# A third inner product of seven in the gated projection, with partial sums put back into PSUM by ScalarE

## The chip, the cores and the metric

One core of a Trainium2 chip. The metric is the device time of one launch in microseconds. Five engines work beside each other, each in its own order and joined by semaphores: TensorE (PE, with its weight loads as PEld), VectorE (DVE), ScalarE (ACT), GpSimd (POOL) and SyncE (SP, which here issues DMAs). Everything is float32. The times of the kernel before are from 3 runs; every other number is from one profiled execution.

## The reference

A graph network on 1024 nodes of 512 features: a normalisation, a graph convolution, four layers, a second graph convolution, and sums with the input. A layer is an attention over a condition and then this block, the part that the change touches:

```python
u = _ln(h, ln3_w[i], ln3_b[i]) @ geglu_w[i] + geglu_b[i]     # 1024x512 @ 512x4096
val, gate = jnp.split(u, 2, axis=-1)
f = val * jax.nn.gelu(gate, approximate=False)               # 1024x2048
h = h + f @ ffo_w[i] + ffo_b[i]                              # 1024x2048 @ 2048x512
```

At the end, `x + (... + relu(layernorm(x)))` is needed once more; the kernel prepares that sum ("base") in eight blocks of 128 rows during the layers and keeps it in DRAM.

## The kernel before

**Sevens.** Most large products are made by Winograd's form of Strassen's scheme: a product of 2x2 blocks takes 7 block products in place of 8, with sums of blocks ahead of them (of weights, mostly on POOL) and sums of results behind them (on VectorE). The block products are numbered 0 to 6 in the order of `order7`.

**Rounds and quads.** The gated projection of a layer `l` goes in `R` = 4 rounds `r`, each for 512 value and 512 gate columns. The outer seven of a round has the blocks val/gate halves by node halves; its left blocks (`left[0..6]`, weights and their sums `ges`) are made by `geglu_weights` on POOL as soon as the round before has made its last sum (`geglu.last`, tile `fs`), its right blocks are `ln3T` and `ln3S`. A `Quad` is 128 of the 512 columns, `c` = 0 to 3: each outer block product of a quad is two matmuls 128x512 into one PSUM bank. Round 0 takes the quads one after the other (`Quad.rest`). Behind each round `ffn_out` multiplies the result `fT` by 512 rows of the output weights (`fa` to `fd`).

**Pairs.** In rounds 1 to 3 quads go in pairs, `p` = 0 (quads 0 and 2) and `p` = 1 (quads 1 and 3). For two of the outer block products, numbers 5 and 6 (`INNER`), a pair makes its four matmuls 128x512 as a seven of its own: `Pair.seven(i)` issues seven matmuls 128x256 into two banks, `ge` (halves a and b) and `gf` (halves c and d). It has two parts, divided by a `yield`:

- products 0 into a, 5 into b, 6 into c, 4 into d; ScalarE copies a to SBUF (L1025), VectorE adds b (L1027), c (L1029) and d (L1031) to that,
- products 1 onto a, 3 onto c, 2 onto d; ScalarE copies a (L1034), VectorE adds c (L1036) and d (L1038).

The results are two SBUF tiles `gw`, one for each quad of the pair. The blocks of blocks that this needs are made on POOL: the left ones by `inner_lefts` right behind `geglu_weights` (tiles `gi`), the right ones once a layer by `inner_right_of` during round 0 (tile `wos`, free at that time).

`Pair.run` weaves the two sevens with the outer products 0 and 4 of both quads, which are ordinary wide matmuls into banks `ga` and `gd`. VectorE adds `ga` and the results of the sevens in SBUF (L1052, L1061). `Quad.end` then makes the products 3, 2 and 1 (banks `gc`, `gd`, `ga`) and the gates: g1 and g0 are sums of a bank and an SBUF tile (L964, L968), gelu on ScalarE (L933), then value times gate (L971 to L975).

**What sets the order.** The tile framework gives every engine its own queue, orders instructions ahead of time by its own estimates, so that matmuls of one step can stand among those of another, and puts in the semaphores. PSUM has eight banks of 128x512, given out from one pool (`bank`). Weights are in 36 buffers (`slot`), loaded by SP; 512-wide scratch tiles are in 10 buffers (`t512`).

**Base blocks.** In rounds 1 to 3 of layer 0 and round 1 of layer 1, two blocks of x each are loaded again (`fetch_x`), normalised by ScalarE, added to the bias and to x by POOL, and written to DRAM through SP's queue (`base_of`).

Of the kernel before, what the change touches and what calls it, by code (L numbers as in the profile page):

```python
# [8 lines left out]
F32 = mybir.dt.float32  # L9
# [5 lines left out]
OP = mybir.AluOpType  # L15
AX = mybir.AxisListType

P = 128
# [5 lines left out]
def gnn_kernel(  # L24
# [46 lines left out]
    slots = ctx.enter_context(tc.tile_pool(name="slots", bufs=36))  # L71
    work = ctx.enter_context(tc.tile_pool(name="work", bufs=10))
    hpool = ctx.enter_context(tc.tile_pool(name="hpool", bufs=1))
    rows = ctx.enter_context(tc.tile_pool(name="rows", bufs=2))
    small = ctx.enter_context(tc.tile_pool(name="small", bufs=4))
    dram = ctx.enter_context(tc.tile_pool(name="dram", bufs=1, space=bass.MemoryType.DRAM))
    psum = ctx.enter_context(tc.tile_pool(name="psum", bufs=8, space=bass.MemoryType.PSUM))
# [14 lines left out]
    def bank(name):  # L92
        return psum.tile([P, 512], F32, tag="bank", name=name)

    def t512(name, dtype=F32):
        return work.tile([P, 512], dtype, tag="t512", name=name)

    def slot(name):
        return slots.tile([P, 2, 512], F32, tag="slot", name=name)
# [10 lines left out]
            )  # L110
        return w

    def load_row(vec, offset, name):
        t = rows.tile([P, D], F32, tag="row", name=name)
        nc.sync.dma_start(
            t, bass.AP(tensor=vec.tensor, offset=vec.offset + offset, ap=[[0, P], [1, D]])
        )
        return t
# [790 lines left out]
    class Quad:  # L909
# [49 lines left out]
        def end(self):  # L959

            n, c, bias = self.n, self.c, gcols[:, self.cv:self.cv + 1]
            pc, pd = bank(f"gc_{n}"), self.d
            g1 = t512(f"g1_{n}")
            nc.vector.tensor_tensor(g1, pd, self.u3, OP.add)  # L964
            self.gate(g1, n)
            self.product(3, pc, True)
            g0 = t512(f"g0_{n}")
            nc.vector.tensor_tensor(g0, pc, self.u3, OP.add)  # L968
            self.gate(g0, n)
            self.product(2, pd, False)  # L970
            nc.vector.scalar_tensor_tensor(self.u2, pd, bias, self.u2, OP.add, OP.add)  # L971
            f0, f1 = (self.fT[i][c // 2][:, c % 2, :] for i in range(2))
            nc.vector.tensor_tensor(f1, self.u2, g1, OP.mult)
            self.product(1, self.a, False)
            nc.vector.scalar_tensor_tensor(f0, self.a, bias, g0, OP.add, OP.mult)  # L975

# [6 lines left out]
    def inner_right(t, y, t1, t2, t3, t4):  # L983

        b11, b12, b21, b22 = (y[:, k, n * M:(n + 1) * M] for k in range(2) for n in range(2))
        for to, of, less in ((t1, b12, b11), (t3, b22, b12), (t2, b22, t1), (t4, b21, t2)):
            t.tensor_tensor(to, of, less, OP.subtract)
        return [b11, b21, b22, t4, t1, t2, t3]

    INNER = (5, 6)  # L990

    def inner_lefts(l, r, left):
        rooms = [t512(f"gi_{l}_{r}_{i}") for i in range(3)]
        rooms = [x[:, i * M:(i + 1) * M] for x in rooms for i in range(2)]
        return {i: inner_left(nc.gpsimd, left[i], *rooms[3 * n:3 * n + 3])
                for n, i in enumerate(INNER)}

    def inner_right_of(n, right):
        rooms = [wos[:, 2 * n + k, i * M:(i + 1) * M] for k in range(2) for i in range(2)]
        return inner_right(nc.gpsimd, right[INNER[n]], *rooms)  # L1000

    class Pair:

# [4 lines left out]
        def seven(self, i):  # L1010

            n, p = f"{self.n}_{i}", self.p
            left, right = (x[i] for x in self.inner)
            e, f = bank(f"ge_{n}"), bank(f"gf_{n}")
            a, b, c, d = e[:, :M], e[:, M:], f[:, :M], f[:, M:]
            t = acc_tile(f"gt_{n}")
            to = self.w = [acc_tile(f"gw{q}_{n}") for q in range(2)]
            s1, u2 = t[:, :M], t[:, M:]

            def product(k, to, start):  # L1020
                nc.tensor.matmul(to, left[k][:, p * P:(p + 1) * P], right[k], start=start,
                                 stop=True, skip_group_check=True)

            product(0, a, True)
            nc.scalar.copy(s1, a)  # L1025
            product(5, b, False)
            nc.vector.tensor_tensor(u2, b, s1, OP.add)  # L1027
            product(6, c, True)
            nc.vector.tensor_tensor(s1, c, u2, OP.add)  # L1029
            product(4, d, False)  # L1030
            nc.vector.tensor_tensor(to[1][:, M:], d, s1, OP.add)  # L1031
            yield
            product(1, a, False)
            nc.scalar.copy(to[0][:, :M], a)  # L1034
            product(3, c, False)
            nc.vector.tensor_tensor(to[1][:, :M], c, u2, OP.add)  # L1036
            product(2, d, False)
            nc.vector.tensor_tensor(to[0][:, M:], d, u2, OP.add)  # L1038
            yield

        def run(self, sums, beside):
            q0, q1 = self.quads
            for q in self.quads:
                q.a = bank(f"ga_{q.n}")
            q0.product(0, q0.a, True)
            steps = self.seven(5)
            next(steps)
            q1.product(0, q1.a, True)
            next(steps)
            for q, w in zip(self.quads, self.w):  # L1050
                q.u2 = w
                nc.vector.tensor_tensor(w, q.a, w, OP.add)  # L1052
            steps = self.seven(6)
            next(steps)
            for q in self.quads:
                q.d = bank(f"gd_{q.n}")
            q0.product(4, q0.d, True)
            next(steps)
            for q, w in zip(self.quads, self.w):
                q.u3 = w  # L1060
                nc.vector.tensor_tensor(w, w, q.u2, OP.add)  # L1061
            q1.product(4, q1.d, True)
            for q in self.quads:
                q.end()
                sums(q.c)
            beside(self.p)
# [196 lines left out]
    for l in range(L):  # L1263
# [119 lines left out]

        last = l == L - 1
        lnT = None
        kept = slot(f"kept_{l}")
        fetched, rights = {}, {}

# [14 lines left out]
        for r in range(R):  # L1403
            if r:
                wff = out_weights(nc.gpsimd, l, r, raw_out)
            else:
                raw_out = load_out(l, 0)
            if r + 1 < R:
                raw = load_geglu(l, r + 1)
            beside = lambda c: None  # L1410
            if r:
                fT, fS, quads = pairs_of(l, r, left, right, (lefts, rights))
                nb = 2 * (l * (R - 1) + r - 1)
                if nb < NB:
                    if nb == 0:
                        bias_out = load_row(gcn_out_b, 0, "bias_out")
                        nc.gpsimd.tensor_tensor(x_shift, x_mean.rearrange(
                            "p a (b c) -> p (a b) c", c=2)[:, :, 0], x_root, OP.mult)
                        nc.gpsimd.tensor_scalar(x_shift, x_shift, -1.0, None, OP.mult)
                    fetch_x(nb)  # L1420
                    fetch_x(nb + 1)
                    beside = lambda p: base_of(nb + p)
            else:
                wff = []

                def beside(c):
                    if c == 2:
                        wff.extend(out_weights(nc.vector, l, 0, raw_out))
                    elif c < 2:
                        with waiting_for(quads[c].last, mybir.EngineType.Pool):  # L1430
                            rights[INNER[c]] = inner_right_of(c, right)

            fT = geglu(quads, fT, fS, not r, beside)
            if r + 1 < R:
                raw_out = load_out(l, r + 1)
                with waiting_for(geglu.last, mybir.EngineType.Pool):
                    left = geglu_weights(l, r + 1, *raw)
                    lefts = inner_lefts(l, r + 1, left)
                    if not r:
                        for nb in range(NB - 2, NB):  # L1440
                            add_bias(nb)
                for s in range(2):
                    ffn_out(l, r, s, fT, wff, kept)
            else:
                lnT = [slots_of(2, f"ln2T_{l + 1}_{i}") for i in range(2)]
                if last:
                    w_out, base = load_last()
                else:
                    projections = load_projections(l + 1)
                ffn_out(l, r, 0, fT, wff, kept)  # L1450
                ready_first(l + 1, [0, 1, 4, 5])
                ffn_out(l, r, 1, fT, wff, kept)
                turn_first(l + 1, [0, 1, 4, 5])
                left_to_turn = [2, 3, 6, 7]
                ready_first(l + 1, left_to_turn[:2])
# [58 lines left out]
```

## Time and profile before

| | us |
|---|---|
| median of 3 runs | 2515.99 (2515.88 to 2517.99) |
| the profiled execution | 2517.15 |
| its span in the profile | 2515.4 |
| PE busy | 2488.1 |
| DVE busy | 1487.5 |
| POOL busy | 619.7 |
| ACT busy | 534.0 |

A MATMUL row of the trace is half of a float32 matmul, with its end modelled; the distance from one start to the next is what PE spends on it. PEld is the load of the stationary operand ahead of each half. A bracket at a row's end gives the idle time of its engine just before, and what ended it. Lines (L1021 and so on) are those of the kernel before; all matmuls of quads and of the other large products have the line of the helper `multiply`, L302.

### The profile page before, as it was taken

To read this page: it belongs to the slowest core of one execution; us is meant where nothing else is said; L and a number is where in the kernel's file an instruction comes from. 1 tells how busy PE (TensorE), PEld (TensorE's weight loads), DVE (VectorE), ACT (ScalarE), POOL (GpSimd) and SP (SyncE) were. 2 spreads that over 40 slices of the span, in tenths; PEclk is the share of its full clock that TensorE was granted. 3 is DMA by queue.
4 is the path that set the end of the run, shared out by engine and by line. 5 is a ranking of instruction groups with operands and counts; after the bars stand their busy time and mean duration, and the time that the engine had idled before them with its cause. 6 is when DMAs were issued, how large, how long until landed. Compare 5 with 4: busy or idle time off the path is not lost. (4 is left out here: it accounts for less than half of the span.)

```text
span 2515.4 us, 33075 instructions
## 1 busy us (share of the span) xinstructions
PE 2488.1 (99%) x12752; PEld 1821.3 (72%) x12752; DVE 1487.5 (59%) x3298; ACT 534.0 (21%) x1318; POOL 619.7 (25%) x581
## 2 busy tenths in 40 slices
PE   8999999999999999999999999999999999999998
PEld 5778886666668887566677888566677888566665
DVE  9655565566764555666574555655574555665561
ACT  7322222111112222111112222211112222211111
POOL 1322233444220113432420113133401112233300
PEclk9999999999999999999999999999999999999999
DMA  6302231121211112020202211110121112111210
GB/s 180 131 30 93 93 120 58 47 67 34 105 59 61 58 64 68 28 81 17 96 30 76 72 64 56 46 42 26 51 76 59 60 59 68 43 42 51 84 34 34
DMA packets 69380, 161.06 MB, mean 64 GB/s; under 512 B 5768, under 2 KB 6096, under 8 KB 69216
## 3 DMA queue, kind: packets, MB, share of 16 engines
q1 hardware_dynamic: 67120, 153.44, 18.7%
q0 software_dynamic: 1376, 4.30, 0.5%
q8 instruction: 105, 1.72, 0.3%
q10 hardware_dynamic: 720, 1.11, 0.1%
q14 instruction: 59, 0.48, 0.1%
HBM read 135.76 MB, written 23.07 MB: 63 GB/s over the span
## 5 line engine op out<-in xcount | busy, mean ns | idle before, releaser
L302 PE MATMUL ga<-ln3T,wval 128*128 128x512 f32 x512 | 245.6, 593 | 0.0
L302 PEld LDWEIGHTS ga<-ln3T,wval 128*128 128x128 f32 x512 | 96.0, 190 | 89.5 <-issue 85.1
L933 ACT ACTIVATE g<-g,gcols 128x512 f32<-128x512 f32 x128 | 87.3, 716 | 329.6 <-DVE g L946 112.6
L777 ACT ACTIVATE pr<-sc,nmax 128x256 f32<-128x256 f32 x256 | 118.2, 474 | 176.7 <-DVE nmax L772 176.7
L302 PE MATMUL gd<-ln3S,ges 128*128 128x512 f32 x256 | 128.1, 592 | 0.0
L302 PE MATMUL pa_v<-wv,ct 128*128 128x256 f32 x512 | 123.1, 379 | 0.0
L220 POOL TENSOR_TENSOR ges<-wgate,wgate 128x1024 f32<-128x1024 f32 x16 | 37.7, 2354 | 342.6 <-DVE fs L1087 329.0
L302 PE MATMUL fa<-wff,fT 128*128 128x256 f32 x512 | 121.6, 379 | 0.0
L302 PE MATMUL gd<-ln3T,ges 128*128 128x512 f32 x256 | 120.7, 594 | 0.6 <-DVE g L964 0.6
L302 PE MATMUL pc_v<-wv,ct 128*128 128x256 f32 x512 | 121.0, 379 | 0.0
L302 PE MATMUL pd_v<-wvs,ct 128*128 128x256 f32 x512 | 121.0, 379 | 0.0
L302 PE MATMUL pc_k<-ct,wk 128*128 128x256 f32 x512 | 120.9, 379 | 0.0
L302 PE MATMUL pd_k<-ct,wks 128*128 128x256 f32 x512 | 120.9, 379 | 0.0
L302 PE MATMUL gc<-ln3S,wgate 128*128 128x512 f32 x256 | 120.3, 592 | 0.0
L302 PE MATMUL pa_k<-ct,wk 128*128 128x256 f32 x480 | 116.2, 385 | 0.0
L302 PEld LDWEIGHTS fa<-wff,fT 128*128 128x128 f32 x512 | 97.3, 190 | 21.8 <-issue 9.1
L302 PEld LDWEIGHTS pc_k<-ct,wk 128*128 128x128 f32 x512 | 97.3, 190 | 13.2
L302 PEld LDWEIGHTS pd_k<-ct,wks 128*128 128x128 f32 x512 | 97.3, 190 | 13.2
L302 PEld LDWEIGHTS pd_v<-wvs,ct 128*128 128x128 f32 x512 | 97.3, 190 | 13.2
L302 PEld LDWEIGHTS pa_v<-wv,ct 128*128 128x128 f32 x512 | 97.1, 190 | 13.5 <-issue 0.4
L302 PEld LDWEIGHTS pc_v<-wv,ct 128*128 128x128 f32 x512 | 95.7, 190 | 12.2
L302 PEld LDWEIGHTS pa_k<-ct,wk 128*128 128x128 f32 x480 | 88.7, 190 | 21.3 <-issue 10.4
(354 smaller groups left out, 4971.5 us busy)
## 6 DMA issues: line engine op xcount, KB each, us to landing
ct<-cond_dram SPq DMA_DIRECT2D x72, 512.0 KB, 4.4
wval<-in_L_gnn_geglu_w_dram SPq DMA_DIRECT2D x32, 512.0 KB, 4.3
wgate<-in_L_gnn_geglu_w_dram SPq DMA_DIRECT2D x32, 512.0 KB, 4.8
wff<-in_L_gnn_ffo_w_dram SPq DMA_DIRECT2D x32, 512.0 KB, 4.0
cond_dram<-ct SPq DMA_DIRECT2D x24, 512.0 KB, 3.2
cond<-in_L_gnn_cond_dram SPq DMA_DIRECT2D x32, 256.0 KB, 4.6
ct<-cond_dram SPq DMA_DIRECT2D x24, 256.0 KB, 5.3
wk<-in_L_gnn_Wk_dram SPq DMA_DIRECT2D x8, 512.0 KB, 4.7
```

What stands on the lines that cost most here:

```text
L220: t.tensor_tensor(s1, a21, a22, OP.add)
L302: nc.tensor.matmul(at, left[:, k, l0:l1], right[:, k, r0:r1], start=start and n == 0 and k == 0, stop=n == len(cols_of) - 1 and k == 1, sk ...
L777: nc.scalar.activation(pr3[:, a, :], ps3[:, a, :], AF.Exp, bias=nmax[:, a:a + 1], accum_out=tot[:, a:a + 1])
L933: nc.scalar.activation(pre, pre, AF.Gelu, bias=gcols[:, cg:cg + 1])
```

## The change

Outer product 0 also becomes an inner seven in rounds 1 to 3, so that a pair has three: `INNER` is (0, 5, 6). The wide matmuls of product 0 are left out. The two banks of each seven, free once its results are in SBUF, stay with the two quads and are used again: ScalarE copies a sum from SBUF into each (`nc.scalar.copy(q.a, q.w1)` and the like, six copies 128x512 a pair), and later outer products are added onto it without a start. The banks of seven 0 take product 0's result and then product 1; those of seven 5 take u2 and then products 4 and 2; those of seven 6 take u2 and then product 3. With u2 already in the banks, `Quad.end` needs one VectorE operation less, and the two SBUF sums L1061 go.

```diff
         def end(self):
...
-            pc, pd = bank(f"gc_{n}"), self.d
+            pc, pd = self.c_, self.d
             g1 = t512(f"g1_{n}")
-            nc.vector.tensor_tensor(g1, pd, self.u3, OP.add)
+            nc.vector.tensor_tensor(g1, pd, self.w7, OP.add)
             self.gate(g1, n)
-            self.product(3, pc, True)
+            self.product(3, pc, False)
             g0 = t512(f"g0_{n}")
-            nc.vector.tensor_tensor(g0, pc, self.u3, OP.add)
+            nc.vector.tensor_tensor(g0, pc, self.w7, OP.add)
             self.gate(g0, n)
             self.product(2, pd, False)
-            nc.vector.scalar_tensor_tensor(self.u2, pd, bias, self.u2, OP.add, OP.add)
             f0, f1 = (self.fT[i][c // 2][:, c % 2, :] for i in range(2))
-            nc.vector.tensor_tensor(f1, self.u2, g1, OP.mult)
+            nc.vector.scalar_tensor_tensor(f1, pd, bias, g1, OP.add, OP.mult)
...
-    INNER = (5, 6)
+    INNER = (0, 5, 6)
...
         def run(self, sums, beside):
-            q0, q1 = self.quads
+            first = self.seven(0)
+            next(first)
+            for q, to, w in zip(self.quads, self.banks, self.w):
+                q.a, q.w1 = to, w
+            sixth = self.seven(5)
+            next(sixth)
+            for q, to, w in zip(self.quads, self.banks, self.w):
+                q.d, q.u2 = to, w
+            next(first)
             for q in self.quads:
-                q.a = bank(f"ga_{q.n}")
-            q0.product(0, q0.a, True)
-            steps = self.seven(5)
-            next(steps)
-            q1.product(0, q1.a, True)
-            next(steps)
-            for q, w in zip(self.quads, self.w):
-                q.u2 = w
-                nc.vector.tensor_tensor(w, q.a, w, OP.add)
-            steps = self.seven(6)
-            next(steps)
+                nc.scalar.copy(q.a, q.w1)
+            next(sixth)
             for q in self.quads:
-                q.d = bank(f"gd_{q.n}")
-            q0.product(4, q0.d, True)
-            next(steps)
-            for q, w in zip(self.quads, self.w):
-                q.u3 = w
-                nc.vector.tensor_tensor(w, w, q.u2, OP.add)
-            q1.product(4, q1.d, True)
+                nc.vector.tensor_tensor(q.u2, q.a, q.u2, OP.add)
+                nc.scalar.copy(q.d, q.u2)
+            last = self.seven(6)
+            next(last)
+            for q, to, w in zip(self.quads, self.banks, self.w):
+                q.c_, q.w7 = to, w
+            next(last)
+            for q in self.quads:
+                nc.scalar.copy(q.c_, q.u2)
+            for q in self.quads:
+                q.product(4, q.d, False)
             for q in self.quads:
                 q.end()
                 sums(q.c)
```

The rest makes room for it. `inner_lefts` makes the sums for three blocks (five scratch tiles for three), `inner_right_of` too, with one more slot a layer (`gr`) for the new one. The base blocks move to round 0, two in every layer: their loads stand in SP's queue behind the next round's weights, `base_of` is called behind the second and third quad, and the bias row (`bias_out`, in its own single buffer) is loaded once ahead of the rounds of layer 0; the pool of rows has one buffer a tag in place of two.

```diff
+                more = slot(f"gr_{l}")
+                for nb in (2 * l, 2 * l + 1):
+                    fetch_x(nb)
+
                 def beside(c):
+                    with waiting_for(quads[c].last, mybir.EngineType.Pool):
+                        if c == 0:
+                            rights[0] = inner_right_of(0, right, more)
+                        elif c < 3:
+                            i = INNER[c]
+                            rights[i] = inner_right_of(i, right, wos[:, 2 * c - 2:2 * c, :])
+                            base_of(2 * l + c - 1)
                     if c == 2:
                         wff.extend(out_weights(nc.vector, l, 0, raw_out))
```

More of the change, by code (lines that the diff above doesn't have):

```diff
@@ L73, in gnn_kernel @@
     hpool = ctx.enter_context(tc.tile_pool(name="hpool", bufs=1))
-    rows = ctx.enter_context(tc.tile_pool(name="rows", bufs=2))
+    rows = ctx.enter_context(tc.tile_pool(name="rows", bufs=1))
     small = ctx.enter_context(tc.tile_pool(name="small", bufs=4))
@@ L111, in load_w, with load_row @@
         return w
-    def load_row(vec, offset, name):
-        t = rows.tile([P, D], F32, tag="row", name=name)
+    def load_row(vec, offset, name, tag="row"):
+        t = rows.tile([P, D], F32, tag=tag, name=name)
         nc.sync.dma_start(
@@ L988, in inner_right @@
         return [b11, b21, b22, t4, t1, t2, t3]
-    INNER = (5, 6)
+    INNER = (0, 5, 6)
     def inner_lefts(l, r, left):
-        rooms = [t512(f"gi_{l}_{r}_{i}") for i in range(3)]
+        rooms = [t512(f"gi_{l}_{r}_{i}") for i in range(5)]
         rooms = [x[:, i * M:(i + 1) * M] for x in rooms for i in range(2)]
@@ L996, in inner_lefts, with inner_right_of @@
                 for n, i in enumerate(INNER)}
-    def inner_right_of(n, right):
-        rooms = [wos[:, 2 * n + k, i * M:(i + 1) * M] for k in range(2) for i in range(2)]
-        return inner_right(nc.gpsimd, right[INNER[n]], *rooms)
+    def inner_right_of(i, right, room):
+        rooms = [room[:, k, j * M:(j + 1) * M] for k in range(2) for j in range(2)]
+        return inner_right(nc.gpsimd, right[i], *rooms)
     class Pair:
@@ L1013, in seven @@
             left, right = (x[i] for x in self.inner)
-            e, f = bank(f"ge_{n}"), bank(f"gf_{n}")
+            e, f = self.banks = bank(f"ge_{n}"), bank(f"gf_{n}")
             a, b, c, d = e[:, :M], e[:, M:], f[:, :M], f[:, M:]
@@ L1385, in gnn_kernel @@
         lnT = None
+        if l == 0:
+            bias_out = load_row(gcn_out_b, 0, "bias_out", "last")
+            nc.gpsimd.tensor_tensor(x_shift, x_mean.rearrange(
+                "p a (b c) -> p (a b) c", c=2)[:, :, 0], x_root, OP.mult)
+            nc.gpsimd.tensor_scalar(x_shift, x_shift, -1.0, None, OP.mult)
         kept = slot(f"kept_{l}")
@@ L1412, in gnn_kernel @@
                 fT, fS, quads = pairs_of(l, r, left, right, (lefts, rights))
[L1413 to L1422, printed above, removed]
             else:
                 wff = []
+                more = slot(f"gr_{l}")
+                for nb in (2 * l, 2 * l + 1):
+                    fetch_x(nb)
                 def beside(c):
+                    with waiting_for(quads[c].last, mybir.EngineType.Pool):
[5 more added lines that the diff above has]
+                            base_of(2 * l + c - 1)
                     if c == 2:
                         wff.extend(out_weights(nc.vector, l, 0, raw_out))
-                    elif c < 2:
-                        with waiting_for(quads[c].last, mybir.EngineType.Pool):
-                            rights[INNER[c]] = inner_right_of(c, right)
             fT = geglu(quads, fT, fS, not r, beside)
```

## The prediction

> **What bounds the kernel now.** I read the page first: its list of engines, the slices, the chain that ended last.
>
> ```profile
> span 2515.4 us, 33075 instructions
> ## 1 busy us (share of the span) xinstructions
> PE 2488.1 (99%) x12752; PEld 1821.3 (72%) x12752; DVE 1487.5 (59%) x3298; ACT 534.0 (21%) x1318; POOL 619.7 (25%) x581
> ...
> PEclk9999999999999999999999999999999999999999
> ```
>
> TensorE (PE) is busy for all but 27 us at full granted clock; VectorE (DVE), ScalarE (ACT) and GpSimd (POOL) have room. Fewer matmul columns are time won, and every PE gap is time lost. Next the busy time by stretches, for the stage that changes (layer 0, round r = 2: two pairs, then the output product):
>
> ```profile
> core 0: us, PE busy (x) PEld busy (x) DVE busy (x) ACT busy (x) POOL busy (x), PEclk, DMA share, GB/s
> ...
> 558.64:605.06 46.42, 46.42 (x137) 25.64 (x136) 31.97 (x53) 9.73 (x18) 5.72 (x4) 1.00 0.12 38
> 605.06:629.24 24.18, 24.18 (x114) 21.28 (x113) 11.68 (x18) 0.00 (x0) 19.82 (x16) 1.00 0.04 16
> ```
>
> PE has no gap in it: 46.42 us for two pairs, 70.60 us for the round. There are 12 such rounds (4 layers, r = 1 to 3), so 24 pairs. Last the instructions in order of time inside a pair, to see why the waits of an inner product of seven are hidden:
>
> ```profile
> 493.21 0.59 PE L1021 MATMUL gf<-wos,gi 128*128 128x256 f32 x2
> ...
> 493.84 0.42 DVE L1031 TENSOR_TENSOR gw<-gf,gt 128x256 f32<-128x256 f32 x1 [0.84 <-PE gf L1021]
> ...
> 494.51 0.59 PE L1021 MATMUL gf<-wos,ges 128*128 128x256 f32 x2
> ...
> 495.14 0.42 DVE L1036 TENSOR_TENSOR gw<-gf,gt 128x256 f32<-128x256 f32 x1 [0.87 <-PE gf L1021]
> ...
> 495.37 1.02 PE L302 MATMUL gd<-ln3S,ges 128*128 128x512 f32 x2
> ...
> 495.80 0.19 PEld L1021 LDWEIGHTS gf<-ln3S,gi 128*128 128x128 f32 x1 [0.24 <-DVE gw L1036]
> ```
>
> These are inner products 4, 3 and 2, all into one bank (gf): 4 and 2 into its right half, 3 into its left. The weight load of product 2 waits for L1036, which reads the *left* half, product 3's. So the three go in lockstep with VectorE: product, reading, product, reading. Before, that is free, because a matmul of other work stands between them on PE (gd at 495.37).
>
> **The price of one such step.** A 256-wide product takes 0.4315 us of PE (eight halves between 544.83 and 546.56, 1.73 us); a 512-wide one 0.859 (20 of these and 14 narrow ones make 23.2, half of 46.42). VectorE starts 0.20 after the product's slot ends (493.21 + 0.43 to 493.84) and reads for 0.425. For the last leg, from VectorE's end to PE, I looked for a stretch in which PE truly waits; there is one:
>
> ```profile
> 668.00 0.69 DVE L964 TENSOR_TENSOR g<-gd,gw 128x512 f32<-128x512 f32 x1
> ...
> 668.74 0.30 PEld L302 LDWEIGHTS gd<-ln3T,ges 128*128 128x128 f32 x2 [1.47 <-DVE g L964]
> 668.74 1.98 PE L302 MATMUL gd<-ln3T,ges 128*128 128x512 f32 x4 [0.64 <-DVE g L964]
> ```
>
> VectorE ends at 668.69, PE goes at 668.74, and the four halves take 1.98 where they take 1.88 elsewhere: 0.15 in all. Bounds: 0.05 (the 0.10 not counted) and 0.25 (a whole weight load of 0.19 exposed). A naked step is R = 0.20 + 0.425 + 0.15 = 0.775 us; with one narrow product beside it, 0.775 - 0.43 = 0.34; with a wide one, nothing.
>
> **The change, part by part.** *Removed matmuls.* Outer product 0 was four 512-wide matmuls a pair and becomes seven 256-wide: 4 x 0.859 - 7 x 0.4315 = 0.416 us saved, 0.83 a round, 10.0 in all.
>
> *Order of the matmuls.* The build's order of the changed kernel's instructions decides the rest. Before, a pair offered two inner sevens (14 narrow matmuls) and eight wide ones free to stand among them (products 0 and 4). After, product 0 is itself a seven, product 4 must add onto a bank that ScalarE fills late, so three sevens have mostly each other for cover. In a pair with p = 0 the second half of the first seven is interleaved with the sixth's and with the next pair's first products; then the sixth's products 4, 3 and 2 stand directly behind each other, each waiting for a VectorE reading. I walked the three queues (PE, DVE, ACT) in that order with the rows' durations; done on the kernel before, this gives 70.61 us for the round against 70.60 measured. From the pair's start, p = 0: product 4 at 6.47 to 6.90; its reading 7.10 to 7.53; product 3 at 7.68 (gap 0.77) to 8.11; reading 8.31 to 8.74; product 2 at 8.89 (gap 0.77) to 9.32. In a pair with p = 1 the same two gaps (2 x 0.78) come, and before them three steps of the first seven with one narrow product for cover (3 x 0.34), since its filling products had been taken by the pair before.
>
> *ScalarE's copies* (six 128x512 a pair, SBUF to PSUM). They queue on ACT in front of the start copy (L1025) of the last seven. The first two wait for the first seven's last sum (VectorE 7.49 to 7.92, behind the sixth's reading at 7.10): ACT 8.01 to 9.15, the start copy 9.11 to 9.48, and the last seven's product 5 goes at 9.64, 0.32 after PE is free; the same in p = 1. The other four are covered: product 4 for four wide matmuls, the gates behind L1063 by products 3 and 2. No row shows ScalarE writing PSUM. Nearest: 0.586 for a copy out of PSUM, 0.716 for an activation from SBUF to SBUF, both 512 wide:
>
> ```profile
> L933 ACT ACTIVATE g<-g,gcols 128x512 f32<-128x512 f32 x128 | 87.3, 716 | 329.6 <-DVE g L946 112.6 <-DVE g L964 102.7 <-DVE g L968 97.5
> ...
> L720 ACT COPY s_v<-pa_v 128x512 f32<-128x512 f32 x31 | 18.2, 586 | 152.1 <-PE pa_v L302 152.1
> ```
>
> I take 0.587, being the same operation with one side in PSUM. Below, I allow 0.45, near the 0.474 of a 256-wide exponential; above, 0.716. In the walk these move a round by -0.54 and +0.52 us. [...]
>
> *Gaps in all:* p = 0: 2 x 0.77 + 0.32 = 1.87; p = 1: 2 x 0.78 + 0.32 + 3 x 0.34 = 2.91. A round: 4.78 of gaps less 0.83 saved is 3.95 us longer, 74.55 for 70.60. Twelve rounds: +47.4.
>
> *VectorE* does two SBUF-only sums and two multiplies fewer a pair (2 x 0.72 + 2 x 0.83) and five 256-wide readings more (5 x 0.425): about 1 us less. It has no load problem; only its place in the lockstep counts. The 0.64 us stall at 668.74 goes away (two sums L1061 there took 1.56 and 1.24 instead of 0.69 while POOL ran; they are gone): -0.7 with its 0.10.
>
> *POOL* gets four more 256-wide sums a round, 4 x 0.685 = 2.7 us between a round's last fs and the next pair. Before, its last inner sum ended at 553.65 with the pair at 558.64, now some 557; the block-0 sums stand early, the last ones are needed 9 us into the pair. Cost 0; without that cover, at most 2.7 a round. The four sums on the right side and the base blocks move into round 0, in which a quad's ten wide matmuls last 8.6 us: two activations of 0.80 and POOL's 2.86 a block lie beside them. *SP:* the x loads now precede the second ffo weights, and their base writes wait for POOL until about 463 us in layer 0; those weights are needed by POOL at about 488, 4 us after issue. The bias row's single buffer waits for the same sums as before. The extra slot delays no load past its first use. All 0.
>
> **Sum.** 47.4 - 0.7 = 46.7 us. The profiled execution took 2517.15 us (span 2515.4 and 1.75 around it), 1.2 above the median of 2515.99; on the median: 2562.7 us.
>
> [...] The lockstep is what the row at 495.80 shows. [...] Were halves guarded singly, the first seven's three steps in p = 1 would vanish (1.03 a round, 12.4 in all, leaving +34), while the sixth's gaps would come back at ScalarE's start copy, which is late on its own: product 5 goes at 9.64 either way.
>
> **Rivals.** *The waits stay hidden* and only the saved columns count: 2515.99 - 10.0 - 0.7 = 2505.3. For it: before, the same waits cost nothing in 24 pairs. Against: there a gd, ga or gc matmul stood between; the order of the changed kernel has none at the sixth. It decides when a round's gaps fall under the 0.83 us saved: with the four naked steps alone, at R of some 0.2 us. 5%. *ScalarE sets the pace:* copies at 0.716 and the last leg at 0.25: a round is 75.70, 5.1 longer, +61 - 0.7: 2576. For it: ACT's queue holds six copies and four gates a pair in order. Against: ACT stays under half busy. 17%. *Cheap copies, quick release* (0.45 and 0.05): a round is 73.51, 2.9 longer: +34, 2550. 12%. *A load or POOL arrives late*, the 2.7 us exposed: 2562.7 + 32 = 2595; POOL's rows speak against it. 2%. That the gaps are real and of the size summed: 64%.
>
> **How the numbers follow.** The likeliest case gives 2562.7. The range takes in the two neighbours with their ends, 2548 to 2580, and leaves the hidden-wait case and a late load outside. A measurement of this kernel can tell about 0.2% (5 us) from no change. Slower: 64 + 17 + 12 + 2 = 95%, less 2 for sizes I cannot see: 93%; faster 5%; same 2%.
>
> **What would show it.** In the changed profile: PE gaps before gf of the sixth seven of 0.77 us, two a pair, released by L1031 and L1036; a gap of about 0.3 at the last seven's ge, released by ScalarE; three of 0.34 in p = 1; a round of 74.5 us; the PSUM copies near 0.59. Wrong, if a round is under 71 us, if PE's idle total stays near 27 us instead of about 84, or if gaps sit elsewhere (at gd adds, or before a round's first ge on POOL).

## The result, and the profile after

The changed kernel takes 2595.34 us (2594.46 to 2596.48) against 2516.88 of the kernel before: 78.5 us more, a ratio of 1.0312 (95% interval 1.03 to 1.0325). The forecast was 2562.7, so the direction was right and some 32 us of the loss were not foreseen. The runs below find 35.7 us in round 0 and the output product behind it, where the forecast had written zeros, and 42.7 of the forecast 46.7 in the rounds 1 to 3. A version built from what they show takes 2506.0 us, faster than both kernels.

The page first, engines and slices:

```profile
span 2592.5 us, 33702 instructions
...
PE 2515.9 (97%) x12896; PEld 1842.2 (71%) x12896; DVE 1469.1 (57%) x3322; ACT 631.1 (24%) x1510; POOL 670.6 (26%) x645
```

PE's idle time has grown from 27.3 to 76.6 us. But its busy time has grown too, by 27.8 us, with fewer matmul columns to do. So a part of the loss is in matmuls that take longer, and the idle total alone will not find it. The busy time by stretches (columns as before) has round r = 2 of layer 0, its two pairs and then its output product, and a stretch behind round 0 that came out of reading the clock:

```profile
571.25:622.16 50.91, 48.67 (x153) 27.77 (x152) 28.69 (x55) 16.47 (x32) 2.39 (x2) 1.00 0.03 10
622.16:645.47 23.31, 23.31 (x109) 20.52 (x108) 11.52 (x18) 0.00 (x0) 20.42 (x19) 1.00 0.27 88
489.36:496.19 6.83, 5.33 (x13) 4.26 (x14) 3.27 (x5) 0.00 (x0) 6.38 (x6) 0.50 0.69 202
```

A round takes 50.91 + 23.31 = 74.22 us, for 70.60 before and 74.55 forecast; the same round of another layer agrees within 0.01. In the third row PEclk is 0.50: for 6.83 us TensorE had half its clock. The instructions in order of time inside the pair (p = 0), at the place forecast for the naked steps:

```profile
577.72 0.59 PE L1021 MATMUL gf<-wos,gi 128*128 128x256 f32 x2
...
578.36 0.42 DVE L1031 TENSOR_TENSOR gw<-gf,gt 128x256 f32<-128x256 f32 x1 [0.97 <-PE gf L1021]
...
578.83 0.70 PE L1021 MATMUL gf<-wos,ges 128*128 128x256 f32 x2 [0.52 <-DVE gw L1031]
...
579.57 0.42 DVE L1036 TENSOR_TENSOR gw<-gf,gt 128x256 f32<-128x256 f32 x1 [0.46 <-PE gf L1021]
...
580.05 0.70 PE L1021 MATMUL gf<-ln3S,gi 128*128 128x256 f32 x2 [0.52 <-DVE gw L1036]
580.24 0.36 ACT L1025 COPY gt<-ge 128x256 f32<-128x256 f32 x1
...
580.75 0.67 PE L1021 MATMUL ge<-wos,gi 128*128 128x256 f32 x2
```

Product, reading, product, reading, as forecast. Product 4 to product 3 is 578.83 - 577.72 = 1.11 us where a slot is 0.43, and the halves then stand 0.10 farther apart (0.70 for 0.59): 0.78 a step. The last seven's product 5 comes late by 0.70 - 0.53 = 0.17, and its halves by 0.08 more.

The waits, PE's longest, show what was not forecast:

```profile
PE fc L302 <- DVE hall L1117: 16.2, 4, 4.1
PE gf L1021 <- DVE gw L1036: 12.4, 24, 0.5
PE gf L1021 <- DVE gw L1031: 12.4, 24, 0.5
...
PE gd L302 <- DVE g L946: 3.6, 4, 0.9
PE fd L302 <- DVE fs L1089: 2.6, 4, 0.7
```

The gf rows are the lockstep. The first row, and the last two, come four times: once a layer, in round 0 and its output product. In order of time, layer 0:

```profile
484.91 1.89 PE L302 MATMUL fa<-wff,fT 128*128 128x256 f32 x8
...
488.81 1.26 POOL L1329 TENSOR_TENSOR hall<-hall,ffb 128x512 f32<-128x512 f32 x1
...
490.11 0.69 DVE L1117 TENSOR_TENSOR hall<-fc,hall 128x512 f32<-128x512 f32 x1 [11.21 <-POOL hall L1329]
...
490.86 3.78 PE L302 MATMUL fc<-wffs,fT 128*128 128x256 f32 x8 [4.05 <-DVE hall L1117]
```

L1329 is `add_bias`, the output product's bias added into `hall` for the last two node blocks (L1326 in the kernel before). Before, POOL did it ahead of most of the weight sums:

```profile
471.02 1.27 POOL L1326 TENSOR_TENSOR hall<-hall,ffb 128x512 f32<-128x512 f32 x1
...
476.87 1.27 POOL L1326 TENSOR_TENSOR hall<-hall,ffb 128x512 f32<-128x512 f32 x1
```

Now the second one stands behind fifteen sums, at 488.81. VectorE's addition of fc needs it and waits 11.2 us, everything behind it in VectorE's queue waits too, the banks are not given back, and PE stands still for 4.05 us. Then eight halves of fc take 3.78 us where eight of fa took 1.89: the halved clock.

### The profile page after: what moved, and what is told of

It is laid out like the page before. It is cut to its first block, busy times and chain, and to the rows that moved or that the text cites. A ratio compares the mean times of both kernels' runs of the same rounds, so it can differ in the third digit from the quotient of the medians.

```text
span 2592.5 us, 33702 instructions
## 1 busy us (share of the span) xinstructions
PE 2515.9 (97%) x12896; PEld 1842.2 (71%) x12896; DVE 1469.1 (57%) x3322; ACT 631.1 (24%) x1510; POOL 670.6 (26%) x645
## 3 DMA queue, kind: packets, MB, share of 16 engines
q10 hardware_dynamic: 720, 1.11, 0.1%
## 5 line engine op out<-in xcount | busy, mean ns | idle before, releaser
L302 PEld LDWEIGHTS pa_v<-wv,ct 128*128 128x128 f32 x512 | 97.1, 190 | 13.5 <-issue 0.4
L1329 POOL TENSOR_TENSOR hall<-hall,ffb 128x512 f32<-128x512 f32 x32 | 41.1, 1290 | 250.8 <-DVE xn_ln L172 250.8
L1025 ACT COPY gt<-ge 128x256 f32<-128x256 f32 x72 | 26.7, 370 | 295.5 <-PE ge L1021 295.5
L848 POOL TENSOR_TENSOR os<-oT 128x256 f32<-128x256 f32 x12 | 8.7, 728 | 320.9 <-DVE oT L823 236.9
L1117 DVE TENSOR_TENSOR hall<-fc,hall 128x512 f32<-128x512 f32 x64 | 44.0, 687 | 79.1 <-POOL hall L1329 44.8
L772 DVE TENSOR_REDUCE nmax<-sc 128x2 f32<-128x512 f32 x128 | 82.9, 679 | 10.2 <-PE sc L765 10.2
```

The costliest lines, as they stand in the source:

```text
L302: nc.tensor.matmul(at, left[:, k, l0:l1], right[:, k, r0:r1], start=start and n == 0 and k == 0, stop=n == len(cols_of) - 1 and k == 1, sk ...
L772: nc.vector.tensor_reduce(nmax, ps3, AX.X, OP.max, negate=True)
L848: t.tensor_tensor(s1, a21, a22, OP.add)
L1117: nc.vector.tensor_tensor(to, halves_of(of), to, OP.add)
L1329: nc.gpsimd.tensor_tensor(h[nb], h[nb], ffb, OP.add)
```

## The experiments

**1. The bias early.** In the changed kernel the two biases are written ahead of the weights' sums.

```diff
                 with waiting_for(geglu.last, mybir.EngineType.Pool):
+                    if not r:
+                        for nb in range(NB - 2, NB):
+                            add_bias(nb)
                     left = geglu_weights(l, r + 1, *raw)
                     lefts = inner_lefts(l, r + 1, left)
-                    if not r:
-                        for nb in range(NB - 2, NB):
-                            add_bias(nb)
```

> The changed kernel with one edit: the bias of the last two node blocks (add_bias, tile hall) is written ahead of the block sums of the weights, so that it stands first in POOL's queue behind round 0. Theory 1 (late bias, and a clock that pays for it): in the changed kernel VectorE's addition into hall waits 11.2 us a layer for POOL's bias, PE stands still for 4.05 us at fc, and the granted clock is half for 3.4 or 6.8 us right behind. With the bias early the 4 x 4.05 = 16.2 us go, and with them the lost clock, 20.5 us at 0.5 = 10.2: about 2569 us, granted clock 1.000. Rival 2 (the clock falls for a reason of its own): only the 16.2 go, 2579, clock still 0.996. Rival 3 (POOL is late as a whole): the block sums now end 2.5 us later, and the first pair of round 1 waits for them instead, some 2.5 us a layer given back or more: 2579 to 2595. The rounds 1 to 3 stay at 74.2 us in all three. [...]

Measured: 2569.25 us, a ratio of 1.0208 to before (1.0191 to 1.0225). PE's wait at fc is gone from the list, and no half clock is left behind round 0 (this profile has 3.41 us of it, at 0.50, at 27.64, in the set-up, where the changed kernel's has none). The two small waits stay, and the rounds are 74.23 as before the edit. So 26.1 us of the 78.5 hang on the place of two POOL instructions a layer: 16.2 of them the stall, and 9.9 are left for the clock, beside 10.2 reckoned from its half-speed stretches. Theory 1 holds.

**2. The base blocks back.** `fetch_x` and `base_of` again in rounds 1 to 3, the bias left late.

```diff
                 fT, fS, quads = pairs_of(l, r, left, right, (lefts, rights))
+                nb = 2 * (l * (R - 1) + r - 1)
+                if nb < NB:
+                    fetch_x(nb)
+                    fetch_x(nb + 1)
+                    beside = lambda p: base_of(nb + p)
...
-                            base_of(2 * l + c - 1)
```

> The changed kernel with the move of the base blocks undone: two blocks in each of the rounds 1 to 3 of layer 0 and in round 1 of layer 1, none in round 0; the bias of the last two node blocks stays where it is. Theory 1 (the third block's inner sums push the bias back): in the build's order the first of the two biases still stands behind nine sums on POOL, so the stall at fc stays near 4 us a layer, and the clock with it; only the small stalls ahead of it (gc 0.25, gd 0.89, fd 0.66 us a layer, where VectorE's sums of fT took 1.75 us instead of 0.68 beside POOL's) shrink, some 7 us: about 2587. Rival 2 (the moved base blocks make POOL late): the stall at fc goes, 2562 to 2570, clock 1.000. Rival 3 (base blocks then collide in the pairs, as in the kernel before, 0.64 us once): no gain, 2595.

Measured: 2587.58 us. The stall at fc is still 3.95 us a layer, and the clock still falls: its mean is 0.997. So the moved base blocks do not make the bias late (rival 2 falls). What is left of theory 1 is the third block's inner sums, the only other work that the change adds to POOL's queue there. That is by elimination: no run takes these sums away and leaves the bias late.

**3. Only the late bias, in the kernel before.**

```diff
-                    if not r:
-                        for nb in range(NB - 2, NB):
-                            add_bias(nb)
+                if not r:
+                    with tc.issue_after(nc.cur_bb.bb.instructions[-1]):
+                        for nb in range(NB - 2, NB):
+                            add_bias(nb)
```

> The kernel before with one edit: the bias of the last two node blocks is made to wait until POOL has issued all block sums of the next round's weights, as it nearly does in the changed kernel. Nothing of the third seven and of ScalarE's copies is in it. Theory 1 (late bias is enough by itself): from the rows of before, POOL's sums from 468.7 on take 4 x 2.32 + 8 x 0.685 + 1.25 = 16.0 us, so the bias ends at some 487.3, VectorE's addition at 488.0, and fc, which PE could begin at 484.6, starts some 3.5 us late: 4 x 3.5 = 14 us, 2530, and if the clock falls behind such a stall up to 10 us more, 2540. Rival 2 (VectorE's order is not in the way, other banks are free): below 2520.

Measured: 2539.18 us, 22.4 more than before (ratio 1.0087, 1.0071 to 1.0104). In order of time:

```profile
488.18 3.78 PE L302 MATMUL fc<-wffs,fT 128*128 128x256 f32 x8 [3.38 <-DVE hall L1114]
```

The stall is 3.38 us, 13.5 in four layers, and the matmuls behind it are slow again (eight halves in 3.78 us, at a granted clock of 0.50 from 487.14 to 493.97); the other 8.9 us are of the size of what the clock lost (a mean granted clock of 0.996 over 2538.6 us: some 10, less what of it lies in the stall itself). A late bias does it without any third seven.

**4. Product 4 free.** Early bias; product 4 in banks of its own, sums of the sevens 5 and 6 on VectorE as before; ScalarE puts back only seven 0's result, and `Quad.end` is that of the kernel before.

```diff
...
             for q in self.quads:
                 nc.vector.tensor_tensor(q.u2, q.a, q.u2, OP.add)
-                nc.scalar.copy(q.d, q.u2)
             last = self.seven(6)
             next(last)
...
+            for q, w in zip(self.quads, self.w):
+                q.u3 = w
+                q.d = bank(f"gd_{q.n}")
+            q0.product(4, q0.d, True)
             next(last)
-            for q in self.quads:
-                nc.scalar.copy(q.c_, q.u2)
-            for q in self.quads:
-                q.product(4, q.d, False)
+            for q in self.quads:
+                nc.vector.tensor_tensor(q.u3, q.u3, q.u2, OP.add)
+            q1.product(4, q1.d, True)
```

> The changed kernel with the early bias of the first run, and with outer product 4 again made into two banks of its own, free to stand anywhere: the sums of the sevens 5 and 6 are made on VectorE in SBUF as in the kernel before, product 3 goes into a bank of its own, and ScalarE only puts seven 0's result into its banks (two copies a pair instead of six). The three sevens stay. Theory 1 (the loss in the rounds is lack of cover): with four wide matmuls a quad back among the sevens the gaps fall from 4.4 us a round to some 0.6, a round from 74.2 to about 70.4: 12 x 3.8 = 46 us less than the first run, about 2523. Rival 2 (the third seven's own lockstep costs, whoever fills the banks): a round stays over 73, 2555 or more. Rival 3 (VectorE's added sums now set the pace): gaps at gd released by L964, a round between.

Measured: 2519.87 us, 49.4 under the first run; a round takes 70.12. With wide matmuls free to stand among the sevens, three sevens a pair are 0.48 us a round cheaper than two. This run alone does not say whether it was the cover or the four copies that are gone.

**5. The copies without the third seven.** The other half of the change, with the early bias: product 0 wide again, products 4 and 3 still added onto banks that ScalarE filled.

```diff
-            first = self.seven(0)
-            next(first)
...
+            for q in self.quads:
+                q.a = bank(f"ga_{q.n}")
+            q0, q1 = self.quads
+            q0.product(0, q0.a, True)
             sixth = self.seven(5)
             next(sixth)
+            q1.product(0, q1.a, True)
...
-            next(first)
-            for q in self.quads:
-                nc.scalar.copy(q.a, q.w1)
             next(sixth)
...
-    INNER = (0, 5, 6)
+    INNER = (5, 6)
```

> The other half of the change alone, with the early bias of the first run: outer product 0 is again four wide matmuls in two banks of its own (INNER is 5 and 6), while the results of the sevens 5 and 6 are still put back into their banks by ScalarE (four copies a pair) and products 4 and 3 are added onto them. Theory 1 (cover): product 0's wide matmuls stand among the sevens again, so the gaps nearly vanish although product 4 still waits for ScalarE: a round of about 70.8 us, 12 x 3.4 = 41 us under the first run, 2525 to 2529. Rival 2 (ScalarE's copies and the products behind them make the gaps): a round of 73 or more, 2555 or more.

Measured: 2527.07 us. The same round as above by stretches, runs 4 and 5:

```profile
560.38:630.50 70.12, 70.03 (x261) 49.06 (x260) 44.55 (x80) 11.65 (x24) 22.45 (x21) 1.00 0.11 37
```

```profile
561.62:632.30 70.68, 70.68 (x249) 46.70 (x248) 36.44 (x62) 12.93 (x24) 20.62 (x17) 1.00 0.09 32
```

Neither half of the change costs more than 0.1 us a round by itself, and PE is busy nearly throughout. Together they cost 3.6. So it is cover: either product 0 or product 4 has to be free to fill the steps. No run has all three sevens and all six copies with cover, so the split between cover and copies rests on these two runs and on the changed kernel's trace, in which ScalarE's start copy makes 0.42 of the gaps of 4.43 us a round and VectorE's readings the rest. Run 5 is still 10 us slower than the kernel before; some 9 of them are in round 0, where its waits at gd, fd and gc are those of the changed kernel (3.6, 2.6 and 1.0 us).

**6. A shorter stall.** The second bias is held two 256-wide sums earlier in POOL's queue than in the changed kernel, by dependencies among the sums of the third block.

```diff
+            if i == 6 and r == 1:
+                add_bias(NB - 2)
+                with tc.issue_after(nc.cur_bb.bb.instructions[-2]):
+                    add_bias(NB - 1)
             lefts[i] = inner_left(nc.gpsimd, left[i], *rooms[3 * n:3 * n + 3])
+            if i == 6 and r == 1:
+                for later in nc.cur_bb.bb.instructions[-3:]:
+                    tc.add_manual_dep(later, add_bias.last.name, ...)
```

> The changed kernel with the second late bias two block sums (2 x 0.685 us) earlier in POOL's queue, so that the stall at fc should be 4.05 - 1.37 = 2.7 us a layer. This asks how long a stall must be for the clock to fall: behind 3.38 us (third run) it fell, behind the 1.69 us between two layers it never does. If it falls behind 2.7 us too: 2595.3 - 5.5 = about 2590 us, granted clock 0.996. If not: the 10.2 us of halved clock go as well, about 2579.5, clock 1.000.

Measured: 2585.97 us, between the two numbers. PE in order of time, and the clock by stretches:

```profile
489.18 3.40 PE L302 MATMUL fc<-wffs,fT 128*128 128x256 f32 x8 [2.68 <-DVE hall L1127]
```

```profile
488.66:492.07 3.41, 2.89 (x7) 2.35 (x8) 2.36 (x4) 0.00 (x0) 3.41 (x4) 0.50 0.59 146
```

The stall is 2.68 us as meant, and in this execution the clock does fall behind it, for 3.41 us in layer 0, where it was 6.83 in the changed kernel. With 3.41 in every layer, which fits the mean granted clock of 0.997, the estimate is 2595.3 - 5.5 - 3.4 = 2586.4. It need not fall each time: one of the four executions took 2583.25 us, with a mean granted clock of 0.999 where the others had 0.997.

**7. Early bias and base blocks in rounds 1 to 3 together** (the edits of runs 1 and 2).

> The early bias and the base blocks in rounds 1 to 3, together (first and second run). If the two costs stand beside each other, their gains add up: the small stalls of round 0 (gc, gd, fd, 1.8 us a layer and what follows them) go from the first run's 2569.25 as they went from the changed kernel in the second, some 8 us: 2561. What is left over the kernel before is then the twelve rounds, 12 x 3.63 = 43.5 us, 2560. If the base blocks collide with VectorE's sums in the pairs instead: up to 2566.

Measured: 2562.71 us, 6.5 under run 1 and within 2 of the sum. What is left is 45.8 us over the 2516.88 of the kernel before.

**8. Three sevens with their cover.** Early bias, base blocks in rounds 1 to 3, the sums as in run 4, and:

```diff
...
+            q0.d = bank(f"gd_{q0.n}")
+            q0.product(4, q0.d, True)
             next(first)
+            last = self.seven(6)
+            next(last)
...
             for q in self.quads:
                 nc.scalar.copy(q.a, q.w1)
             next(sixth)
             for q in self.quads:
                 nc.vector.tensor_tensor(q.u2, q.a, q.u2, OP.add)
...
+            q1.d = bank(f"gd_{q1.n}")
+            q1.product(4, q1.d, True)
             next(last)
...
                         if c == 0:
+                            rights[5] = inner_right_of(5, right, wos[:, :2, :])
                             rights[0] = inner_right_of(0, right, more)
...
+                        elif c == 1:
+                            rights[6] = inner_right_of(6, right, wos[:, 2:, :])
```

> A version that keeps the third seven and gives it its cover: early bias; base blocks in rounds 1 to 3; the right sums of all three blocks made behind the first two quads of round 0 (the third set no longer meets the last sums of fT on VectorE); product 4 in banks of its own, quad 0's issued between the sevens 0 and 5, quad 1's behind the second half of seven 5; the first half of the last seven issued ahead of ScalarE's copies and of the second half of seven 5, so that each lockstep has other products beside it. Sums on VectorE as in the kernel before, ScalarE puts only seven 0's result back. Theory (the saved columns are real and the gaps were the whole loss): a round is 70.60 - 0.83 + 0.05 = 69.8, twelve of them 9.4 us less than before, and the 0.64 us stall at 668 of the kernel before goes: 2507. Rival 2 (base blocks and the four more sums on POOL slow VectorE's SBUF sums in the pairs): a round of 70.1 to 70.6, 2511 to 2517. Rival 3 (the extra sums on POOL come late for the next round): more than 2517.

Measured: 2509.69 us, a ratio of 0.997 (0.9959 to 0.9981), faster than before. A round with base blocks and one without, by stretches:

```profile
559.11:629.76 70.65, 70.25 (x261) 49.06 (x260) 47.68 (x80) 13.29 (x26) 28.30 (x25) 1.00 0.10 30
1142.75:1212.53 69.78, 69.78 (x261) 49.15 (x260) 45.70 (x80) 11.88 (x24) 22.82 (x22) 1.00 0.11 36
```

The eight rounds without base blocks are the theory's 69.8; in the four with them VectorE is busy for 2 us more with the same 80 operations, and PE waits: rival 2, there alone. The total lies between the two forecasts (2507, and 2511 or more).

**9. The base blocks in round 0, behind quads 0 and 1.** The rest is run 8; the lines are set against the changed kernel.

```diff
-                            base_of(2 * l + c - 1)
+                        if c < 2:
+                            base_of(2 * l + c)
```

> As the eighth run (three sevens with their cover, early bias, early right sums), but the base blocks in round 0 as in the changed kernel, behind its first two quads instead of its second and third. In the eighth run the four rounds with base blocks take 70.65 us and the other eight 69.8. Theory (POOL's additions for base blocks slow VectorE's SBUF sums in those rounds, and behind the first two quads of round 0 nothing waits for VectorE): all twelve rounds 69.8, 4 x 0.85 = 3.4 us less and the 0.6 us stall at fd of layer 0, about 2505.5. Rival (what slows those rounds is their ScalarE work or loads, or round 0 pays the same at its gates): 2509 or more.

Measured: 2506.0 us, a ratio of 0.9959 (0.9945 to 0.9972). The rounds are 69.8 in every layer. Since the base blocks moved as a whole, it stays open which of their parts, POOL's additions, ScalarE's activations or the loads, slowed the four rounds of run 8. This beats the kernel before by 10.7 us, and the changed one by 89.

**10. The last seven's first half earlier, the rest as in run 1.**

```diff
             next(first)
+            last = self.seven(6)
+            next(last)
+            for q, to, w in zip(self.quads, self.banks, self.w):
+                q.c_, q.w7 = to, w
             for q in self.quads:
                 nc.scalar.copy(q.a, q.w1)
...
-            last = self.seven(6)
-            next(last)
-            for q, to, w in zip(self.quads, self.banks, self.w):
-                q.c_, q.w7 = to, w
```

> The changed kernel with the early bias and one move in a pair: the first half of the last seven is issued ahead of ScalarE's copies of product 0's result and of the second half of the seven before it; products 4 and 3 still wait for ScalarE's sums in their banks. Theory 1 (the loss is lack of cover, not the order): the steps of the sixth get narrow products beside them, but the last seven then has none left for its own, and the walk through the queues with the rows' durations gives 74.3 us a round: 2569 as in the first run, within 4. Rival 2 (ScalarE's copies standing ahead of the last seven's start copy in its queue hold the sevens apart): a round falls by 2 us or more, 2545 or less.

Measured: 2565.98 us, a round of 74.0. The gf waits for L1036 are gone, others for L1029 have come (4.9 us). Moving cover from one seven to another changes little.

## Why the prediction was right in the rounds and wrong in the sum

*The naked step* (R = 0.775): 0.78. *The last seven's late product 5* (0.32): 0.17 + 0.08 = 0.25 with p = 0, 0.17 with p = 1. *The first seven's three steps in p = 1* (0.34 each): 0.19, 0.35 and 0.35. *ScalarE's copies into PSUM* (0.587, bounds 0.45 to 0.716): 0.583 to 0.596 in the six groups, for instance

```profile
L1063 ACT COPY gf<-gw 128x512 f32<-128x512 f32 x24 | 14.2, 590 | 70.2 <-DVE gw L1038 70.2
```

so neither the dearer nor the cheaper copy came about. *Gaps in all:* 1.81 + 2.62 = 4.43 a round instead of 4.78; less the saved 0.83 that is 3.60, and 74.22 - 70.60 = 3.62 is what the round shows. Twelve of them, less the stall at 668.74, which did go: 42.7 us where the forecast had 46.7. Runs 4, 5 and 10 confirm the reason given (two sorts of filling products taken away at once), runs 8 and 9 that the 0.83 us a round are real once the cover is back.

**The step that failed** is the zero for POOL and for what moves into round 0 (the part that begins "POOL gets four more 256-wide sums a round"). It looked at whether the weight sums would be ready for the next pair. They were. It did not look at what else stands in POOL's queue at that place: the biases, which the build's order now puts behind the new sums, and for which VectorE, and through the banks PE, waits. The rival "a load or POOL arrives late" had 2%, and sought the wait at a pair's start. Its 2595 is the measured time by chance: it adds 32 us of late weight sums to the rounds, and PE waits for no such sum. Nor did the sum have a term for slow matmuls behind a stall. By the runs:

| of the 78.5 us | us | from |
|---|---|---|
| rounds 1 to 3 | 42.7 | the twelve rounds of the trace |
| late bias and halved clock | 26.1 | run 1 |
| base blocks in round 0 | 6.5 | run 7 less run 1 |
| left over in round 0 | 3.1 | 45.8 (run 7) less 42.7 |

The third line is the "All 0" for the base blocks. It was said that two activations and POOL's sums lie beside a quad's ten matmuls. They do, but VectorE does not run unhindered beside them. In order of time, at the end of round 0 of the changed kernel:

```profile
461.20 1.75 DVE L1088 TENSOR_TENSOR fs<-fT,fT 128x512 f32<-128x512 f32 x1
...
462.87 0.68 DVE L946 TENSOR_TENSOR g<-gd,gu 128x512 f32<-128x512 f32 x1
...
463.50 1.78 POOL L1408 TENSOR_TENSOR x_again<-x_again,again 128x512 f32<-128x512 f32 x1
463.61 1.98 PE L302 MATMUL gd<-ln3T,ges 128*128 128x512 f32 x4 [0.89 <-DVE g L946]
```

The sum of fT took 0.68 us at this place before (L1085 there, with POOL idle from 455 to 468):

```profile
461.15 0.68 DVE L1085 TENSOR_TENSOR fs<-fT,fT 128x512 f32<-128x512 f32 x1
```

With POOL adding in SBUF beside it, it takes 1.75, the gate sum queued behind it is late, and PE waits 0.89. In this trace L1088 at 461.20 and L1090 at 464.07, with both inputs in SBUF, took 1.75 beside POOL, and L946 at 462.87, with one of them in PSUM, 0.68. Two rows stand apart: L216 at 460.60 and L1089 at 463.47, with both inputs in SBUF too, took 0.67 and 0.68, each just where one sum of POOL ended and the next began. The forecast had slow rows of this sort before it (the two L1061 of 1.56 and 1.24 us "while POOL ran") and used them only for a stall that goes. What the left-over 3.1 us are was not tried apart; 2.4 of them are waits at gd and gc (0.35 and 0.25 a layer in run 7), where right sums run beside VectorE. It is their place behind the third quad that seems to count, and not that a third block has come: run 5, without one, makes right sums there too and waits 0.23 at gc.

One of the signs named in advance was blind: PE's idle total came to 76.6 us, not far from the 84 forecast, because idle time in round 0 was there instead, and because the profile counts a matmul at half clock, and part of each lockstep gap, as busy (2.24 of a round's 4.43 us of gaps show as idle). The stretches by round and the granted clock told the cases apart.

## What to carry to other kernels

Before an engine's extra work is put at nothing, list all that stands behind it in that engine's queue, and for each of them who waits; the cheap, early-needed instruction that slips behind a long batch is the one that costs. Matmuls that fill another chain's waits are worth more than their columns: take one sort of filler away at a time, and place the rest by hand. A PE stall of a few microseconds in a full kernel should be priced with the slow matmuls behind it: here 2.5 us more behind one of 4.05.

## What was not expected of the hardware

Behind the stalls at fc the clock was halved (granted clock 0.50): in the changed kernel, with 4.05 us of stall in each of the four layers, for 6.83, 3.41, 6.83 and 3.41 us; in layer 0 of run 3 (3.38 us) for 6.83, and of run 6 (2.68 us) for 3.41. For run 2 (3.95 us) the mean granted clock of 0.997 speaks for the same. Behind the idle 1.69 us between layers 0 and 1 of both kernels the granted clock stayed at 1.00. Behind a 4.05 us stall the loss was 9.9 / 4 = 2.5 us more.

The length of a stall alone does not decide. In the set-up of run 9, PE stood idle for 1.89 us and then for 2.36, and the matmuls were slow behind the first only:

```profile
26.22 2.95 PE L462 MATMUL hw_in<-w_in,h0T 128*128 128x512 f32 x4 [1.89 <-ACT h0T L454]
...
86.29 1.97 PE L302 MATMUL pa_kT<-ct,wk 128*128 128x256 f32 x8 [2.36 <-DVE v_deg L134]
```

At the first place the changed kernel, after 1.83 us of idle time and at a granted clock of 1.00, took 1.98 us for the same four halves, where run 9 took 2.95. At the second both took 1.97 for the eight, the changed kernel after 1.94 us. What else decides, no run here shows.
